# Scores of a graph-attention kernel: two pairs of groups by seven half-size products, one list of buffers, three paced queues

## The chip, the cores and the metric

One core of one Trainium2 chip. The metric is the device time of one execution in microseconds (us), given as the median of several runs. Where a ratio is given, it is the mean time of one kernel's fast runs over that of the other's fast runs of the same rounds, so it is not quite the ratio of the medians quoted beside it; the bracket behind it is a 95% interval.

## The reference, cut to what matters

```python
# layer 0: x = layernorm(x + relu(adj @ (max(sign(x), 0) @ sign(w0).T)))     x: 4096 x 512, adj: 4096 x 4096
node_att = softmax(x @ node_w, axis=0)
h = x @ edge_w
e = h @ h.T                                  # symmetric: block (A, B) is block (B, A) turned
e = where(adj > 0, e, NEG_BIG)
edge_att = softmax(e, axis=1)                # over rows: block (B, A) has its own minima and sums
output = adj * (node_att * edge_att) @ (x @ weight) + bias
# then layernorm(x + output)
```

The kernel cuts the 4096 rows into 8 groups of 512 (`NG = 8`, `W = 512`), each of four blocks of 128 rows (`BG = 4`). A pair (A, B) of groups is 512 x 512 scores. Only 28 pairs off the diagonal and 8 on it are multiplied; the mirror block is made by turning (transposing) on TensorE. This stage, the stage of the scores, is the one that is changed. It lasts a quarter of the run.

## The kernel before

The stage of the scores, with cuts marked. `later` is one queue of following work, of which four entries are emitted after each row.

```python
blk = ctx.enter_context(tc.tile_pool(name="blk", bufs=11))
adjp = ctx.enter_context(tc.tile_pool(name="adjp", bufs=2))
def some(n):
    for _ in range(min(n, len(later))):
        later.popleft()()
class Scores:
    # load(): two adjacency tiles of 128 x 2048, [...]
    def prepare(self):
        for a in self.a:
            nc.vector.tensor_scalar(a, a, 0.0, NEG_BIG, ALU.is_le, ALU.mult)      # L332
    def stats(self, a, i, r, c, s):                                             # one row block: mask, minimum, exp
        nc.vector.tensor_tensor_reduce(e, e, s, -1.0, HUGE, ALU.add, ALU.min, accum_out=nmax_c[...])
        later.append(lambda: nc.scalar.activation(e, e, AF.Exp, ...))
    def main(self):
        for i in range(BG):
            # four accumulating matmuls into pe (128 x 512 in PSUM)             # L356
            nc.scalar.copy(s[:, i, lo * P :], pe[:, lo * P :])                  # L363
            if not diag:
                self.stats(self.a[0], i, A, B, pe)
            some(4)
            later.appendleft(lambda i=i: self.turn(s, t, i))                    # turned one i later
```

The helper `seven` was there already (the stage of h and the aggregation use the same seven-product scheme):

```python
def m1(ps, q, c11, c12, c21, c22): nc.scalar.copy(c21, ps)
def u2(ps, q, c11, c12, c21, c22): nc.vector.tensor_add(c12, c21, ps)           # L104
def u3(ps, q, c11, c12, c21, c22):
    nc.vector.tensor_add(c22, c21, ps)                                          # L110
    nc.vector.tensor_add(c22, c22, banks[2][q])                                 # L111
    after(q, 3)
# m2: ScalarE copy; m4, m3: one VectorE addition each (L119, L123)
```

TensorE needs the PSUM bank that `u2` reads for a later product, and the turn of a row waits for `u3`'s result.

## Time and profile before

| | before |
|---|---|
| time, median of 4 runs | 2026.82 us (2026.47 to 2028.78) |
| stage of the scores (first score product to first aggregation product) | 514.2 us |
| instructions of that stage on TensorE x their rate | 507.5 us |
| TensorE idle in that stage | 4.5 us |
| from the first aggregation product to the end | 896.4 us |

The second part of the table is worked out from the trace: each TensorE instruction of the stage by its nominal spacing (0.43 us for one of 128 x 512, as eight take 3.44 us at full rate; for narrower ones the trace shows 0.32 us with 384 columns, 0.22 with 256 and 0.11 with 128), then the idle time that the trace gives, then a remainder (2.2 us), in which instructions ran below their rate.

### The profile page before, as it was taken

To read this page: it belongs to the slowest core of one execution; us is meant where nothing else is said; L and a number is where in the kernel's file an instruction comes from. 1 tells how busy PE (TensorE), PEld (TensorE's weight loads), DVE (VectorE), ACT (ScalarE), POOL (GpSimd) and SP (SyncE) were. 2 spreads that over 40 slices of the span, in tenths; PEclk is the share of its full clock that TensorE was granted. 3 is DMA by queue.
4 is the path that set the end of the run, shared out by engine and by line. 5 is a ranking of instruction groups with operands and counts; after the bars stand their busy time and mean duration, and the time that the engine had idled before them with its cause. 6 is when DMAs were issued, how large, how long until landed. Compare 5 with 4: busy or idle time off the path is not lost.

```text
span 2025.5 us, 17689 instructions
## 1 busy us (share of the span) xinstructions
PE 2004.4 (99%) x6268; PEld 1108.3 (55%) x6268; DVE 1243.5 (61%) x1759; ACT 691.5 (34%) x1195; POOL 401.5 (20%) x485
## 2 busy tenths in 40 slices
PE   9999999999999999999999999999999999999997
PEld 4888888888544454545555444444444444444443
DVE  3555555556534554445545897786759775977634
ACT  4333333333113666666666521131221220222100
POOL 0243333334300000000001111140124111321101
PEclk9999999999999999999999999999999999999999
DMA  9566566565009786867767887765666765685421
GB/s 328 186 220 203 196 216 210 201 209 173 29 0 351 260 302 229 308 231 272 280 257 265 330 329 258 250 248 198 249 237 251 260 246 201 227 283 201 172 70 62
DMA packets 118153, 455.73 MB, mean 225 GB/s; under 512 B 10288, under 2 KB 10288, under 8 KB 93488
## 3 DMA queue, kind: packets, MB, share of 16 engines
q0 software_dynamic: 48128, 241.20, 31.6%
q1 hardware_dynamic: 69360, 212.36, 31.6%
q8 instruction: 49, 0.80, 0.2%
q10 hardware_dynamic: 576, 1.05, 0.1%
q14 instruction: 40, 0.33, 0.0%
HBM read 355.99 MB, written 98.57 MB: 224 GB/s over the span
## 4 chain that ended last, share of the span: by engine, by line
PE 96%; DMA 3%; DVE 1%; ACT 0%; issue 0%; SPq 0%; ACTq 0%; POOLq 0%; POOL 0%; DVEq 0%
PE ps L479 38%; PE pe L356 21%; PE acc L209 11%; PE acc L208 11%; PE po L531 5%; PE seven L89 5%; PE pt L377 3%; DMA a<-in_adj_dram 2%; PE pw L181 1%; PE pt L238 1%; DMA xt<-in_x_t_dram 1%; DVE lo L205 0%; PE ptm L405 0%; DMA xb<-x_d 0%; ACT a L342 0%
## 5 line engine op out<-in xcount | busy, mean ns | idle before, releaser
L356 PE MATMUL pe<-hT 128*128 128x512 f32 (+3 forms) x1152 | 475.5, 557 | 0.0
L479 PE MATMUL ps<-q,lop 128*128 128x512 f32 x1024 | 446.9, 592 | 0.0
L208 PE MATMUL acc<-xw,hi 128*128 128x512 f32 x1024 | 401.6, 392 | 0.0
L209 PE MATMUL acc<-xw,lo 128*128 128x512 f32 x1024 | 399.4, 390 | 0.6 <-DVE lo L205 0.5
L479 PE MATMUL ps<-t,lop 128*128 128x512 f32 x768 | 332.9, 592 | 0.0
L479 PEld LDWEIGHTS ps<-q,lop 128*128 128x128 f32 x1024 | 193.9, 190 | 240.8 <-issue 237.0
L356 PEld LDWEIGHTS pe<-hT 128*128 128x128 f32 x1152 | 205.0, 191 | 184.0 <-issue 174.8
L434 ACT ACTIVATE q<-q 128x2048 f32<-128x2048 f32 x64 | 122.3, 1911 | 407.8 <-DVE q L431 394.2
L205 DVE TENSOR_TENSOR lo<-at,hi 128x1024 fp32r<-128x1024 f32 x128 | 168.7, 1318 | 147.1 <-ACT hi L203 147.1
L479 PEld LDWEIGHTS ps<-t,lop 128*128 128x128 f32 x768 | 145.9, 190 | 183.7 <-issue 180.3
L440 DVE SCALAR_TENSOR_TENSOR q<-ac,q 128x512 f32<-128x512 f32 x256 | 198.9, 830 | 53.6 <-ACT q L434 39.1
L203 ACT CAST hi<-at 128x1024 fp32r<-128x1024 f32 x128 | 134.6, 1052 | 272.6 <-PE acc L208 271.3
L209 PEld LDWEIGHTS acc<-xw,lo 128*128 128x128 f32 x1024 | 192.3, 188 | 41.0 <-DVE lo L205 1.7
L208 PEld LDWEIGHTS acc<-xw,hi 128*128 128x128 f32 x1024 | 192.3, 188 | 39.3
L338 DVE CUSTOM_DVE_ANT_0 a<-a,pe 128x512 f32<-128x512 f32 x112 | 76.7, 687 | 206.9 <-ACT s L363 206.9
L342 ACT ACTIVATE a<-a,nmax_c 128x512 f32<-128x512 f32 x256 | 183.5, 718 | 45.8 <-DVE nmax_c L338 45.5
L483 DVE TENSOR_TENSOR over<-over,ps 128x512 f32<-128x512 f32 x168 | 113.6, 681 | 107.8 <-PE ps L479 107.7
L431 DVE CUSTOM_DVE_ANT_1 q<-q,mrow 128x2048 f32<-128x2048 f32 x64 | 148.5, 2325 | 40.3 <-DMA q<-s_d 36.2
L363 ACT COPY s<-pe 128x512 f32<-128x512 f32 (+2 forms) x144 | 77.7, 543 | 138.4 <-PE pe L356 120.3
L531 PE MATMUL po<-over 128*128 128x512 f32 x256 | 115.9, 600 | 3.7 <-DVE xb L540 3.7
L425 POOL DMA_DIRECT2D ac<-in_adj_t_dram x64 | 48.8, 763 | 325.3 <-DVE q L440 253.4
L377 PEld LDWEIGHTS pt<-ident,s 128*128 128x128 f32 x496 | 62.1, 141 | 68.7 <-issue 57.7
(107 smaller groups left out, 1553.8 us busy)
## 6 DMA issues: line engine op xcount, KB each, us to landing
at<-in_adj_t_dram SPq DMA_DIRECT2D x64, 1024.0 KB, 5.1
ac<-in_adj_t_dram POOLq DMA_DIRECT2D x64, 1024.0 KB, 6.7
a<-in_adj_dram SPq DMA_DIRECT2D x64, 1024.0 KB, 7.5
q<-s_d POOLq DMA_DIRECT2D x64, 1024.0 KB, 7.8
lop<-lop_d SPq DMA_DIRECT2D x112, 512.0 KB, 4.1
s_d<-s POOLq DMA_DIRECT2D x36, 1024.0 KB, 4.8
s_d<-t POOLq DMA_DIRECT2D x28, 1024.0 KB, 6.2
xb<-in_x_dram SPq DMA_DIRECT2D x32, 256.0 KB, 3.1
```

What stands on the lines that cost most here:

```text
L203: nc.scalar.copy(hi, aq)
L205: nc.vector.tensor_sub(lo, aq, hi.bitcast(F32))
L208: nc.tensor.matmul(acc, hi[:, c, :], xw[:, kb, :], start=(kb == 0), stop=False)
L209: nc.tensor.matmul(acc, lo[:, c, :], xw[:, kb, :], start=False, stop=(kb == NB - 1))
L342: lambda: nc.scalar.activation(e, e, AF.Exp, bias=nmax_c[:, b, c : c + 1], scale=-1.0, accum_out=sum_c[:, b, c : c + 1])
L356: nc.tensor.matmul(pe[:, lo * P :], hT[:, k, ts(A * BG + i, P)], hT[:, k, (B * BG + lo) * P : (B + 1) * W], start=(k == 0), stop=(k == KD ...
L377: nc.tensor.transpose(pt[:, j, :], s[:, i, ts(j, P)], ident)
L431: nc.vector._custom_dve(TENSOR_ADD_SAT, out=q, in0=q, in1=mrow.unsqueeze(1).to_broadcast([P, BG, W]), s0=0.0, s1=-HUGE)
L434: nc.scalar.activation(q, q, AF.Exp)
L440: nc.vector.scalar_tensor_tensor(qc, a[:, :, c, :], 0.0, qc, ALU.max, ALU.mult)
L479: nc.tensor.matmul(ps, lop[:, c, ts(h, P)], rop[m][:, c, :], start=(c == 0), stop=(c == BG - 1))
L531: nc.tensor.matmul(po, (lower if k // 2 else upper)[:, k % 2, ts(i, P)], w1_s[:, k, :], start=(k == 0), stop=(k == KD - 1),)
```

## The change

Two pairs (A, B) and (A, B+1) are made together by seven products of half size with five additions out of PSUM per half, instead of eight products. That saves TensorE one instruction in eight. The sums of the left and right operands are made by GpSimd. Eleven plus two buffers become one list of 13 that are handed back by count; the one queue `later` becomes three (turns, rows, exps), from which `tick` emits a little after every half product. The preparation of a tile is no longer emitted one unit ahead but directly ahead of the tile's first row. The core of the diff:

```diff
-    blk = ctx.enter_context(tc.tile_pool(name="blk", bufs=11))
-    adjp = ctx.enter_context(tc.tile_pool(name="adjp", bufs=2))
+    free = deque(slots_p.tile([P, BG, W], F32, name=f"slot{n}") for n in range(13))
+    def tick():
+        now[0] += 1
+        if turns and turns[0][0] <= now[0]:
+            turns.popleft()[1]()
+        for _ in range(1 + (len(stats) > 6)):
+            if stats:
+                stats.popleft()()
+        for _ in range(1 + (len(exps) > 4)):
+            if exps and exps[0][0] <= now[0]:
+                exps.popleft()[1]()
[...]
+        def row(self, i, s):
+            if self.fresh:
                 nc.vector.tensor_scalar(a, a, 0.0, NEG_BIG, ALU.is_le, ALU.mult)
+                self.fresh = False
             nc.vector.tensor_tensor_reduce(e, e, s.buf[:, i, :], -1.0, HUGE, ALU.add, ALU.min, ...)
[...]
+        def written(self, i):
+            stats.append(lambda: self.here.row(i, self.s))
+            turns.append((now[0] + 2, lambda: self.turn(i)))
[...]
+    class Couple:
+        def operands(self):
+            if B not in Couple.right:            # once per column of couples, 128 x 1024 each
+                nc.gpsimd.tensor_sub(t1, r12, r11)
+                nc.gpsimd.tensor_sub(t2, r22, t1)
+                nc.gpsimd.tensor_sub(t3, r22, r12)
+                nc.gpsimd.tensor_sub(t4, r21, t2)
+            nc.gpsimd.tensor_add(s1, l21, l22)   # per couple, 128 x 512 each
+            nc.gpsimd.tensor_sub(s2, s1, l11)
+            nc.gpsimd.tensor_sub(s3, l11, l21)
+            nc.gpsimd.tensor_sub(s4, l12, s2)
+        def main(self, between):
+            seven(left, right, [...], follow)
[...]
+    for B in range(0, NG, 2):
+        units += [Couple(A, B) for A in range(B)]
+        units += [Single(B, B), Single(B, B + 1), Single(B + 1, B + 1)]
```

## The prediction

What it calls the lock is this, in the trace of the kernel before: four operations of VectorE that read two SBUF operands (L440) took 9.33 us beside three GpSimd operations of 6.94 us together, and 2.48 us without them. The name stands for these longer durations; what causes them, no trace shows.

> **What bounds the kernel now.** I read the page first (busy shares, slices, chain), then the stage of the scores by windows, then its timeline instruction by instruction, then the waits of the other engines.

> ```profile
> span 2025.5 us, 17689 instructions
> PE 2004.4 (99%) x6268; PEld 1108.3 (55%) x6268; DVE 1243.5 (61%) x1759; ACT 691.5 (34%) x1195; POOL 401.5 (20%) x485
> PEclk9999999999999999999999999999999999999999
> PE 96%; DMA 3%; DVE 1%; ACT 0%; issue 0%; SPq 0%; ACTq 0%; POOLq 0%; POOL 0%; DVEq 0%
> L356 PE MATMUL pe<-hT 128*128 128x512 f32 (+3 forms) x1152 | 475.5, 557 | 0.0
> 614.90:1129.20 514.30, 509.85 (x1652) 262.42 (x1651) 260.53 (x615) 329.16 (x783) 39.40 (x72) 1.00 0.76 278
> ```

> TensorE works without a break (99%, full clock) and the chain is TensorE for 96%. The last line is the window of the score stage: length, then busy PE, weight loads, DVE, ACT, POOL, clock, DMA share, GB/s. 509.85 of 514.30 us are TensorE; DVE is at 51%, ACT at 64%. A busy TensorE need not be at its rate, so the timeline decides:

> ```profile
> 800.84 3.60 PE L356 MATMUL pe<-hT 128*128 128x512 f32 x8
> 804.27 0.60 PE L377 MATMUL pt<-ident,s 128*128 128x128 f32 x4
> 804.71 3.60 PE L356 MATMUL pe<-hT 128*128 128x512 f32 x8
> ```

> One product of 128x512 is two instructions (1152 = 2 x 576 products). Eight of them start 3.43 us before the transposes that follow, and the windows 663 to 741 and 741 to 1104 are busy to the last hundredth (78.00 of 78.00, 363.00 of 363.00): 0.429 us per instruction is the rate, and the time goes down only with the number of instructions. The only idle of TensorE in the stage is at its start, 2.91 and 1.54 us (waits on ACT's copy, which stood behind DVE and the first adjacency loads):

> ```profile
> 639.33 1.14 PE L377 MATMUL pt<-ident,s 128*128 128x128 f32 x8 [2.91 <-ACT s L363]
> 659.22 0.66 PE L377 MATMUL pt<-ident,s 128*128 128x128 f32 x4 [1.54 <-ACT s L363]
> ```

> [...] in the aggregation stage:

> ```profile
> 1334.34 9.33 DVE L440 SCALAR_TENSOR_TENSOR q<-ac,q 128x512 f32<-128x512 f32 x4 [1.05 <-DMA ac<-in_adj_t_dram]
> 1334.36 6.94 POOL L504 TENSOR_TENSOR over<-over 128x1024 f32<-128x1024 f32 x3
> L213 DVE CUSTOM_DVE_ANT_0 scr<-xb,nw_b x32: 693/1246/1251, 56.3 to 522.6; 128x512 f32<-128x512 f32 x32
> ```

> Four operations that elsewhere take 2.48 us together took 9.33 us, longer by just about the 6.94 us of three POOL operations; DVE did not get in between them. L213 is the row operation of the score stage in form, and doubles (693 to 1246 ns) beside POOL. [...] Here a 128x512 subtraction took 1306 ns on POOL alone (L262) and 0.69 us on DVE: 1.9x. [...] a ready copy stood behind an exp that waited for DVE.

> **The change, part by part.** *Products.* There are 28 pairs off the diagonal and 8 on it. The new order makes 12 couples (2+4+6) out of 24 pairs; 4 pairs and the diagonal stay. Two pairs cost 2 x 16 = 32 products; seven products of half size are 7 x 2 x 2 = 28, at the same width of 512. Saved: 4 products, 8 instructions x 0.429 = 3.43 us per couple, x 12 = **41.2 us**, 96 instructions. All of it lies on the path. The transposes stay (496). A couple takes 56 x 0.429 = 24.0 us and eight groups of transposes at 0.44 us = 3.5 us: 27.5 us, where two pairs took 8 x 3.87 = 31.0 us. Floor: 2026.6 - 41.2 = 1985.4 us, a ratio of 0.980.

> *DVE.* Each couple adds ten additions out of PSUM (five per half). Such an addition is 0.69 us, 0.61 back to back by the same helper in the stage of h (L104 to L123 show 688, 687, 686, 687, 684 ns). Rows come every 0.615 us back to back (starts 798.00, 798.62, 799.23, 799.84), a tile's preparation is 1.22 us (L332). Per couple: 16 x 0.615 + 4 x 1.22 + 10 x 0.61 = 20.8 us of 27.5, 76%; two pairs had 14.7 of 31.0, 47%.

> *POOL.* Each couple needs four sums of 128x512, about 1.3 us each: 5.2 us. Each of three new columns (B = 2, 4, 6) needs four more of 128x1024, 2.34 us each (the fastest of L273): 9.4 us. None had to be made before. All 16 rows of a couple now read two SBUF operands (half read PSUM before)[...]: 20.8 + 5.2 = 26.0 us of 27.5, 95%.

> *ACT.* It loses four of eight copies per couple (-2.3 us): 16 exps at 0.705 (starts 798.84, 799.55, 800.25), 8 turn copies at 0.59, 4 copies at 0.58 make 18.3 us of 27.5, 67%. Not a bound.

> *Slack.* Before, a row was turned one i later, 3.4 us after its product ended, and only an ACT copy lay between. Now it is turned one half-product later, 1.72 us, and six of eight rows come through DVE. For the row of the fourth product two additions must fit: product's end + 0.2 us (in the stage of h the additions start at 539.61 and 543.05, their products end at 539.41 and 542.85) + 1.3 us = 1.5 us. With a free DVE it fits by some 0.2 us. With DVE behind it doesn't, and TensorE waits in order.

> *Buffers.* 11 + 2 buffers of 8 KB per partition become one list of 13; a couple holds about nine at once. In the aggregation this loads the masks two at a time as before, and TensorE had no idle there: I expect 0 there.

> **What is given back (estimates).** Placing the queues by hand: the stores of a pair come a few half-products before the sums in POOL's order, so the sums run roughly around half-products 4 to 8, when DVE has rows and preparations and then the two tight pairs of additions. Of 5.2 us of lock, DVE's idle takes most; I count 1 us of TensorE wait per couple: **+12 us**. At a new column POOL's chain to the second product's operands (four of 2.34, two of 1.3: 12 us) starts in the diagonal unit before it, some 9 us before TensorE needs it, and earlier as far as POOL runs ahead; DVE is held out meanwhile. 2 us each: **+6 us**. At the change of stage the first block's q load is issued one step before its shift; in-order DVE and ACT would stand behind a load (7.8 us median landing) that was issued 9 to 13 us ahead before (1095.44 and 1099.91 for a shift at 1108.86). The products' copies wait behind that: **+4 us**. The start has two loads before it instead of four, and the first unit waits for one tile: of the 4.45 us idle perhaps **-3 us** (some comes back). Sum: 1985.4 + 12 + 6 + 4 - 3 = 2004; I take **2003 us**, 1.2% less.

> **Rivals.** (A) *All of it arrives*: 1985 us, or 1983 with the better start. For it: every engine but TensorE stays under its capacity, the row queue is bounded and doubles its pace above six, and the 5.2 us of POOL may fall into DVE's idle; the same seven products ran in the stage of h at 0.429 us per instruction. Against it: there DVE had little else to do. (B) *DVE under the lock becomes the bound*: if sums block DVE right ahead of additions, each couple loses 2.5 us or more, 30 us, and the columns and the change of stage 15 to 20: 2020 to 2030 us, nothing gained. For it: 95% and 9.33 us for 2.48 us of work above. Against: a TensorE wait lets DVE catch up[...]. (C) *Buffers or transfers*: with 13 buffers taken, emission must drain queues early and loads wait for exps; the same bytes in 473 us make 302 GB/s where the stage had 278 and single slices 351. It would show as DVE waiting for in_adj; some us at most.

> **Range and chances.** A and B bracket the result; the paced queues speak for the better half, the lock for the worse. 1986 to 2020 us should hold it 8 times in 10. Faster by over 2% means under 1986.1 us, which needs the whole floor: 0.14. Slower by over 2% would need more than 80 us of new stalls: 0.03. Within 2%: 0.83.

> **What would show it.** Right: 1056 instructions in the two score lines together (672 more on the helper's L89 row), and the stage's window about 490 us; busy DVE there near 340 us plus time in which rows last over 1 us beside POOL; TensorE idle, ended by DVE additions, ahead of transposes in the couples. Step "lock" is wrong if rows stay at 687 ns or if no TensorE idle follows; "columns" is wrong if TensorE has no gap at the first couples of a column; "change of stage" is wrong if TensorE runs through from the last score into the first block. A time under 1988 us means that slack was enough; one above 2020 us that DVE paces the couples.

## More of the kernel before

The prediction shows the main lines. Two more are needed later. The list of waits has one for VectorE (the columns: waiting line, releaser, us in total, times, longest):

```profile
DVE a L332 <- DMA a<-in_adj_dram: 27.8, 17, 10.8
```

and the page's list of transfers gives what an adjacency tile takes from issue to landing (last number, us):

```profile
a<-in_adj_dram SPq DMA_DIRECT2D x64, 1024.0 KB, 7.5
```

So VectorE already stood 27.8 us, up to 10.8 us at a time, with a preparation at the head of its queue whose tile had not landed. It cost TensorE only the 4.5 us at the start of the stage; after that TensorE never came to wait for VectorE here.

## The result, and the profile after

The changed kernel takes **2097.92 us** (median of 4, 2096.48 to 2100.87) against 2026.82 us, ratio 1.0351 [1.0333, 1.0369]: 3.5% slower, outside the predicted range of 1986 to 2020 us. From the page of the changed kernel:

```profile
span 2099.1 us, 17645 instructions
...
PE 2003.9 (95%) x6170; PEld 1101.2 (52%) x6172; DVE 1340.2 (64%) x1879; ACT 663.1 (32%) x1147; POOL 507.4 (24%) x545
...
PEclk9999999999999998899998999999999999999999
...
PE 81%; DMA 11%; DVE 4%; ACT 3%; issue 1%; POOL 0%; POOLq 0%; DVEq 0%; SPq 0%
...
L359 DVE TENSOR_SCALAR slot<-slot 128x2048 f32<-128x2048 f32 x64 | 90.6, 1417 | 146.2 <-DMA slot<-in_adj_dram 146.0
...
slot<-in_adj_dram SPq DMA_DIRECT2D x64, 1024.0 KB, 12.1
```

Before, the chain that ended last was TensorE for 96% and the clock line (PEclk: the clock that TensorE was granted, in tenths of full speed) had only nines. Now the chain is TensorE for 81%, transfers for 11% and VectorE for 4%; TensorE is idle at times, and the clock line has eights where it had been full. L359 is the preparation of an adjacency tile: VectorE stands 146.0 us in front of it, waiting for the tile to land. The waits, by line:

```profile
DVE slot L359 <- DMA slot<-in_adj_dram: 146.0, 44, 8.6
...
PE seven L89 <- DVE slot L104: 47.1, 12, 7.7
...
PE pt L410 <- DVE slot L111: 17.5, 9, 3.0
...
PE pt L410 <- ACT slot L445: 12.4, 3, 4.6
```

TensorE waits 47.1 us for the additions of `u2`, 17.5 us for those of `u3`. The stage as a window (length, busy PE, PEld, DVE, ACT, POOL, then clock, DMA share and GB/s):

```profile
616.00:1203.50 587.50, 508.89 (x1561) 255.31 (x1560) 364.90 (x737) 302.99 (x739) 131.13 (x130) 0.93 0.65 242
```

| us | before | after | difference |
|---|---|---|---|
| stage of the scores | 514.2 | 587.5 | +73.3 |
| its TensorE instructions at their rate | 507.5 | 467.0 | -40.5 |
| TensorE idle in it | 4.5 | 78.6 | +74.1 |
| remainder: below the rate | 2.2 | 41.9 | +39.7 |
| from there to the end | 896.4 | 895.5 | -0.9 |

So the products were saved as predicted and the aggregation is as it was. (The table has 40.5 us for the predicted 41.2 because six transposes of the kernel before come after its first aggregation product, and so outside the stage; with them it is 41.2.) The loss is TensorE idle and, after it, slow TensorE. One couple shows how (columns: start, duration in us, engine, line, operation, count, and in brackets the idle time before and what ended it):

```profile
1050.01 1.23 DVE L359 TENSOR_SCALAR slot<-slot 128x2048 f32<-128x2048 f32 x1 [2.59 <-DMA slot<-in_adj_dram]
...
1053.60 0.68 DVE L104 TENSOR_TENSOR slot<-slot,seven 128x512 f32<-128x512 f32 x1
...
1057.66 2.50 DVE L359 TENSOR_SCALAR slot<-slot 128x2048 f32<-128x2048 f32 x1 [3.38 <-DMA slot<-in_adj_dram]
...
1060.08 0.67 DVE L104 TENSOR_TENSOR slot<-slot,seven 128x512 f32<-128x512 f32 x1
1060.68 1.21 DVE L359 TENSOR_SCALAR slot<-slot 128x2048 f32<-128x2048 f32 x1
...
1060.81 3.67 PE L89 MATMUL seven<-right,slot 128*128 128x512 f32 x4 [3.45 <-DVE slot L104]
...
1065.35 1.23 DVE L359 TENSOR_SCALAR slot<-slot 128x2048 f32<-128x2048 f32 x1 [3.46 <-DMA slot<-in_adj_dram]
...
1068.04 1.09 PE L410 MATMUL pt<-ident,slot 128*128 128x128 f32 x4 [2.69 <-DVE slot L111]
```

Read it from the middle. The second L104 addition stands behind a preparation. VectorE is idle for 3.38 us because the preparation's tile lands late; the preparation takes 2.50 us (beside a GpSimd sum, 1.22 otherwise); then comes the addition, and TensorE, idle for 3.45 us, goes on 0.7 us after the addition began. Its next four instructions then start 0.85 to 0.90 us apart, where 0.43 is the rate: they run at half rate. The same follows at 1065.35 for `u3`.

Nothing written says that this preparation comes before this addition. In the text of the program it stands directly ahead of its tile's first row. In the order in which the built program holds VectorE's instructions it does not (the number, line and operation of the couple shown above; rows shortened to `L362`, and what each preparation is for added behind it):

```
953 L359 preparation of slot10    its first row is number 1000: 16 rows and 10 additions later
954, 956, 958, 960  L362 rows of slot0
962 L104 addition (u2)
963 L359 preparation of slot11    first row 988: 7 rows and 8 additions later
964 L104 addition (u2)            <- TensorE waits for this one
965 L359 preparation of slot4     first row 1021: 18 rows and 14 additions later
966 L359 preparation of slot7     first row 1016: 16 rows and 13 additions later
967 L110 addition (u3)
968 L111 addition (u3)            <- and for this one
```

A preparation depends on nothing but its tile's load, and the build has put it far ahead. Over the 64 tiles it stands on average 13 rows and 8.3 additions ahead of its first row. In the kernel before it stood nearly 18 rows ahead, but with no addition between.

The loads themselves are not faster for it: they are issued when a buffer comes free, four loads and four stores close together. The window from 1028 to 1072 us in 40 slices, with the share of the DMA engines and their rate:

```profile
DMA  0000000000000899699999999999999991000000
GB/s 0 0 0 0 0 0 0 0 0 0 0 0 0 357 357 238 246 391 272 404 413 434 439 402 391 404 400 410 393 387 458 415 376 37 0 0 0 0 0 0
```

About 22 us at some 380 GB/s, then nothing: a tile lands 12.1 us after its issue (7.5 before), though the stage as a whole moves only 242 GB/s.

### The profile page after: what moved, and what is told of

Same layout as the page of the kernel before. It is cut to its first block, busy times and chain, and to the rows that moved or that the text cites. A ratio compares the mean times of both kernels' runs of the same rounds, so it can differ in the third digit from the quotient of the medians.

```text
span 2099.1 us, 17645 instructions
## 1 busy us (share of the span) xinstructions
PE 2003.9 (95%) x6170; PEld 1101.2 (52%) x6172; DVE 1340.2 (64%) x1879; ACT 663.1 (32%) x1147; POOL 507.4 (24%) x545
## 3 DMA queue, kind: packets, MB, share of 16 engines
q0 software_dynamic: 48128, 241.20, 30.4%
q10 hardware_dynamic: 576, 1.05, 0.1%
## 4 chain that ended last, share of the span: by engine, by line
PE 81%; DMA 11%; DVE 4%; ACT 3%; issue 1%; POOL 0%; POOLq 0%; DVEq 0%; SPq 0%
PE ps L604 37%; PE acc L209 11%; PE seven L89 11%; PE acc L208 11%; DMA slot<-in_adj_dram 10%; PE po L657 5%; PE pe L436 2%; ACT slot L368 2%; PE pt L410 2%; PE pw L181 1%; DVE slot L359 1%; DVE slot L362 1%; PE pt L238 1%; DMA s_d<-slot 1%; ACT slot L411 1%
## 5 line engine op out<-in xcount | busy, mean ns | idle before, releaser
L604 PE MATMUL ps<-slot,lop 128*128 128x512 f32 x1792 | 774.1, 592 | 0.0
L604 PEld LDWEIGHTS ps<-slot,lop 128*128 128x128 f32 x1792 | 339.9, 190 | 425.2 <-issue 414.2
L546 ACT ACTIVATE slot<-slot 128x2048 f32<-128x2048 f32 x64 | 122.0, 1911 | 394.1 <-DVE slot L543 394.1
L552 DVE SCALAR_TENSOR_TENSOR slot<-slot,slot 128x512 f32<-128x512 f32 x256 | 185.9, 779 | 51.2 <-DMA slot<-in_adj_t_dram 37.7
L368 ACT ACTIVATE slot<-slot,nmax_c 128x512 f32<-128x512 f32 x256 | 183.6, 720 | 108.2 <-DVE nmax_c L362 108.1
L362 DVE CUSTOM_DVE_ANT_0 slot<-slot,slot 128x512 f32<-128x512 f32 x256 | 181.3, 740 | 46.1 <-ACT slot L115 28.5
L543 DVE CUSTOM_DVE_ANT_1 slot<-slot,mrow 128x2048 f32<-128x2048 f32 x64 | 158.0, 2473 | 68.0 <-DMA slot<-s_d 66.8
L89 PE MATMUL seven<-right,slot 128*128 128x512 f32 x288 | 143.9, 652 | 47.1 <-DVE slot L104 47.1
L359 DVE TENSOR_SCALAR slot<-slot 128x2048 f32<-128x2048 f32 x64 | 90.6, 1417 | 146.2 <-DMA slot<-in_adj_dram 146.0
L436 PE MATMUL pe<-hT 128*128 128x512 f32 (+3 forms) x384 | 135.0, 500 | 0.0
L89 PEld LDWEIGHTS seven<-right,slot 128*128 128x128 f32 x288 | 57.1, 204 | 122.8 <-issue 65.2
L411 ACT COPY slot<-pt 128x512 f32<-128x512 f32 (+3 forms) x136 | 73.9, 546 | 131.4 <-PE pt L410 110.9
## 6 DMA issues: line engine op xcount, KB each, us to landing
slot<-in_adj_dram SPq DMA_DIRECT2D x64, 1024.0 KB, 12.1
```

The costliest lines, as they stand in the source:

```text
L89: nc.tensor.matmul(banks[bank][q], lop(m, q)[k], rop(m)[k], start=(first and k == 0), stop=(k == K - 1), skip_group_check=not first,)
L362: nc.vector.tensor_tensor_reduce(e, e, s.buf[:, i, :], -1.0, HUGE, ALU.add, ALU.min, accum_out=nmax_c[:, b, c : c + 1])
L368: nc.scalar.activation(e, e, AF.Exp, bias=nmax_c[:, b, c : c + 1], scale=-1.0, accum_out=sum_c[:, b, c : c + 1])
L436: nc.tensor.matmul(pe[:, lo * P :], hT[:, k, ts(p.A * BG + i, P)], hT[:, k, (p.B * BG + lo) * P : (p.B + 1) * W], start=(k == 0), stop=(k ...
L543: nc.vector._custom_dve(TENSOR_ADD_SAT, out=q, in0=q, in1=mrow.unsqueeze(1).to_broadcast([P, BG, W]), s0=0.0, s1=-HUGE)
L552: nc.vector.scalar_tensor_tensor(qc, a[:, :, c, :], 0.0, qc, ALU.max, ALU.mult)
```

## The experiments

Three explanations were open after this reading. **Order**: the preparations stand ahead of TensorE's additions in VectorE's queue, and wait there for their tiles (3.38 us in the couple above, with TensorE idle for 3.45). **Lock**: VectorE's operations last longer beside GpSimd's sums, as the preparation of 2.50 us above (the prediction's main loss). **Supply**: 13 buffers or the transfers are too few. All medians are in us; "before" ran in the same rounds (2026.6 to 2028.2 us). The experiments were made in four sets of rounds on four chips (e1 to e4, e5 to e8, e9 to e11, e12 and e13), so a difference between runs of different sets is uncertain by some 1.5 us.

| run | edit | median | ratio to before | idle + remainder of the stage |
|---|---|---|---|---|
| after | | 2097.92 | 1.0351 [1.0333, 1.0369] | 78.6 + 41.9 |
| e1_pin_prep | preparation kept in written order | 2033.81 | 1.0034 [1.0019, 1.0049] | 37.6 + 17.1 |
| e2_thin_sums | short GpSimd sums | 2100.66 | 1.0357 [1.0340, 1.0374] | 79.1 + 41.6 |
| e3_singles | no couples | 2039.24 | 1.0063 [1.0048, 1.0078] | 7.8 + 7.7 |
| e4_slots14 | a 14th buffer | 2089.74 | 1.0307 [1.0292, 1.0322] | 80.2 + 27.2 |
| e5_pin_turn3 | e1 and a later turn | 2015.27 | 0.9934 [0.9919, 0.9948] | 23.0 + 11.5 |
| e6_pin_thin_sums | e1 and e2 | 2009.00 | 0.9904 [0.9887, 0.9920] | 20.4 + 10.2 |
| e7_turn3 | later turn alone | 2111.18 | 1.0408 [1.0392, 1.0423] | 90.2 + 42.6 |
| e8_pin_singles | e1 and e3 | 2022.67 | 0.9971 [0.9956, 0.9986] | 0.6 + 1.0 |
| e9_pin_turn3_pool | e5, GpSimd in written order | 2034.57 | 1.0037 [1.0023, 1.0052] | 38.4 + 17.6 |
| e10_turn4_pool_first | e9, turn later still, next stage's loads earlier | 2017.14 | 0.9950 [0.9934, 0.9967] | 30.0 + 9.8 |
| e11_turn3_pool_rows_first | e9, rows in written order, loads earlier | 2031.55 | 1.0026 [1.0009, 1.0042] | 36.9 + 12.3 |
| e12_dve_sums | e5, all sums on VectorE | 1988.23 | 0.9802 [0.9789, 0.9816] | 7.3 + 5.9 |
| e13_dve_sums_turn2 | e1, all sums on VectorE | 1989.08 | 0.9803 [0.9791, 0.9815] | 5.0 + 4.8 |

### e1_pin_prep: the preparation alone in its written place

```diff
-                nc.vector.tensor_scalar(a, a, 0.0, NEG_BIG, ALU.is_le, ALU.mult)
+                tc.keep_in_program_order(nc.vector.tensor_scalar(a, a, 0.0, NEG_BIG, ALU.is_le, ALU.mult))
```

> One edit: each preparation of an adjacency tile (one DVE operation on 128x2048) is pinned behind what was written before it on DVE, so that it stands right ahead of its own first row (0.2 rows and 0.5 additions between, mean of 64) and not 13.1 rows and 8.3 additions ahead of it, where the compiler's scheduler put it. Theory ORDER (DVE waits in order at a hoisted preparation for a tile that has not landed, and the additions behind it hold TensorE): 1985 to 2005 us, DVE's wait for in_adj in the score stage from 146 us to under 30, additions no longer end TensorE's idle. Rival LOCK (the POOL sums shut DVE out): over 2070 us. Rival BUFFERS (13 buffers too few, tiles simply come too late): over 2060 us, the wait for in_adj stays over 80 us and only stands ahead of other rows.

Measured: 2033.81 us, 64.1 us less than the changed kernel, by this one line, though not the 1985 to 2005 us that I expected: additions still end TensorE's idle time, those of `u3`. In its built order a preparation is 0.2 rows ahead of its first row on average. Its waits:

```profile
PE pt L410 <- DVE slot L111: 31.0, 9, 5.4
DVE slot L359 <- DMA slot<-in_adj_dram: 5.1, 1, 5.1
```

The 146.0 us of VectorE's waits for tiles are 5.1, with the same buffers and nearly the same landing time (11.9 us), and TensorE no longer waits for L104 at all. So the tiles were not late for their rows, only for the places at which the build had put their preparation. What remains, 31.0 us for L111, is another thing. The same place of a couple in this run:

```profile
1009.17 1.26 POOL L473 TENSOR_TENSOR slot<-hT 128x512 f32<-128x512 f32 x1 [5.55 <-PE seven L89]
...
1009.35 1.62 DVE L362 CUSTOM_DVE_ANT_0 slot<-slot,slot 128x512 f32<-128x512 f32 x1
...
1012.08 1.72 POOL L474 TENSOR_TENSOR slot<-slot,hT 128x512 f32<-128x512 f32 x1
...
1012.59 1.75 DVE L362 CUSTOM_DVE_ANT_0 slot<-slot,slot 128x512 f32<-128x512 f32 x1
...
1014.27 1.90 DVE L362 CUSTOM_DVE_ANT_0 slot<-slot,slot 128x512 f32<-128x512 f32 x1
...
1016.10 1.22 DVE L359 TENSOR_SCALAR slot<-slot 128x2048 f32<-128x2048 f32 x1
...
1017.24 0.68 DVE L110 TENSOR_TENSOR slot<-slot,seven 128x512 f32<-128x512 f32 x1
1017.95 0.69 DVE L111 TENSOR_TENSOR slot<-slot,seven 128x512 f32<-128x512 f32 x1
...
1018.78 1.09 PE L410 MATMUL pt<-ident,slot 128*128 128x128 f32 x4 [2.81 <-DVE slot L111]
```

Rows of 0.69 us take 1.15 to 1.90 us beside GpSimd's sums (1.62, 1.15, 1.75 and 1.90 for the four) and push the two tight additions back; TensorE waits 2.81 us. This is the mechanism of the prediction's rival B, and the time is near the 2020 to 2030 us that it gave.

### e2_thin_sums and e6_pin_thin_sums: the lock, with and without the pin

```diff
+            w = 8 if A else P
-            nc.gpsimd.tensor_add(s1, l21, l22)
+            nc.gpsimd.tensor_add(s1[..., :w], l21[..., :w], l22[..., :w])
             # the other three sums of a couple likewise
```

This makes wrong operands in the couples with A above 0 (the comparison let the result pass, so it can't be used to check such a kernel). The four sums of a couple stay in GpSimd's queue with their waits, but last a fraction.

> The order of DVE is as in the changed kernel, but the four POOL sums of a couple are made on 8 of 128 columns (not for the three first couples); results are wrong on purpose. The POOL time of a couple falls from 5.3 us to about 1. ORDER: 2075 to 2100 us. LOCK: under 2050 us. BUFFERS: 2085 to 2100 us.

Measured: 2100.66 us, no gain at all, with 79.1 us idle as in the changed kernel. As long as the preparations set VectorE's pace, the lock is not what ends last. Together with the pin of e1:

> Preparations pinned as in e1, and the POOL sums on 8 of 128 columns as in e2 (wrong operands on purpose). SLACK-AND-LOCK: without the lock the rows ahead of the first pair of additions take 0.69 us again, DVE is 3 us or more earlier there, the pauses go: 1988 to 2004 us, where the same edit gained nothing (2100.7) with hoisted preparations. Rival (throughput of DVE or the preparation alone): over 2020 us.

Measured: 2009.00 us, 24.8 us below e1, but above the 1988 to 2004 us that I expected. The same edit is worth nothing in one order and 25 us in the other. The trace says where the rest is: of e1's eight pauses of over 2 us for L111, the six of 2.6 to 4.8 us are gone or under 0.8 us, and the two of 5.4 us stand as they were, 5.45 and 5.44 us, beside the sums of 128 x 1024 for the next column, which this edit left at full size.

### e3_singles and e8_pin_singles: the rest of the change without couples

```diff
-        units += [Couple(A, B) for A in range(B)]
+        units += [Single(A, C) for A in range(B) for C in (B, B + 1)]
```

> The new queues, list of 13 and order of units, but every pair by itself with full products (no couples, no sums, no additions out of PSUM). Preparations are hoisted as far as in the changed kernel (16.3 rows). ORDER: nothing that TensorE needs stands behind them except ACT's exps, so 2020 to 2040 us, near the kernel before. LOCK: the same, 2020 to 2030. BUFFERS: the list and the queues cost by themselves, over 2050 us.

Measured: 2039.24 us. Every pair is multiplied in the old way here, with the new queues and the list of 13.

> Every pair by itself as in e3_singles (2039.2 us, 12 above the kernel before), preparations pinned. If those 12 us come from exps and copies on ACT that stand behind rows behind hoisted preparations: 2024 to 2031 us. If the one list of 13 or the pace of the queues costs them: 2036 to 2042 us.

Measured: 2022.67 us. The moved preparations cost even this order 16.6 us; with the pin, queues and buffers by themselves are 0.3% better than the kernel before, with only 0.6 us of TensorE idle in the stage. The buffers and queues by themselves are thus not the fault.

### e4_slots14: one buffer more

```diff
-    free = deque(slots_p.tile([P, BG, W], F32, name=f"slot{n}") for n in range(13))
+    free = deque(slots_p.tile([P, BG, W], F32, name=f"slot{n}") for n in range(14))
-        mrow = pan.tile([P, W], F32, name="mrow")
+        mrow = pan.tile([P, W], F32, name="mrow", bufs=2)
```

> A 14th buffer in the list (room from two of four mrow buffers), nothing else. BUFFERS: under 2065 us, as each tile can be asked for earlier. ORDER: hoisting stays (13.8 rows); loads come a little earlier, 2070 to 2098 us. LOCK: 2090 to 2100 us.

Measured: 2089.74 us, 8.2 us less. VectorE still waits 119.5 us for tiles. Supply is a small part. (The room came from two buffers of the aggregation, which took 898.0 us here against 895.5. Twelve buffers can't be tried: the program's list then never has one free where it needs it, and the build doesn't end.)

### e5_pin_turn3 and e7_turn3: more slack for the turn

```diff
-            turns.append((now[0] + 2, lambda: self.turn(i)))
+            turns.append((now[0] + 3, lambda: self.turn(i)))
```

The turn of a row comes three half products after it, not two. With the pin:

> Preparations pinned as in e1_pin_prep, and each row turned one half-product later (now + 3 for now + 2). In e1 TensorE still stood 31.4 us in 12 pauses of about 2.6 us, one per couple, at the transposes of the first row with two additions; DVE was late there by four rows of 1.15 to 1.90 us beside the four POOL sums and by one preparation. Theory SLACK-AND-LOCK: 2.15 us more slack leaves about 0.5 us of each pause and ends most of the half-clock time after it: 1988 to 2004 us, idle in the score stage under 15 us. Rival: the pauses come from DVE's throughput (additions, rows and preparations over a whole couple), then they only move: over 2020 us.

Measured: 2015.27 us, 18.5 us below e1 and better than both kernels, but above what I expected, with 23.0 us idle. (Nor was it one pause per couple in e1: its trace has eight for L111 of over 2 us, of 2.6 to 5.4, in the 12 couples.) Without the pin:

> The later turn alone, preparations hoisted as in the changed kernel (12.9 rows, 7.7 additions ahead). ORDER: the pauses of 4 to 8 us at additions that stand behind a late tile stay, 2070 to 2098 us. If slack alone were the cause: under 2050 us.

Measured: 2111.18 us, outside what I expected, and 13 us worse than the changed kernel. The additions still stand behind preparations whose tiles have not landed; TensorE waited 60.7 us for L111 here (17.5 before the edit). Why it got worse rather than stayed equal I did not follow further.

### e9, e10, e11: trying to keep GpSimd's sums where they were written

The largest pauses left in e5 were two of 4.9 us, at the last couple of a column, where rows ran beside GpSimd's sums for the next column's right operands. I took their place to be the trouble, and pinned all GpSimd sums to their written order:

```diff
-                nc.gpsimd.tensor_sub(t1, r12, r11)
+                tc.keep_in_program_order(nc.gpsimd.tensor_sub(t1, r12, r11))
                 # and so for all eight GpSimd sums                           (e9, e10, e11)
-            turns.append((now[0] + 3, lambda: self.turn(i)))
+            turns.append((now[0] + 4, lambda: self.turn(i)))               # e10
-            nc.vector.tensor_tensor_reduce(
+            tc.keep_in_program_order(nc.vector.tensor_tensor_reduce(       # e11
```

e10 and e11 also emit the first loads of the next stage ahead of its two panels.

> As e5_pin_turn3 (2015.3 us), and the POOL operations that make a column's and a couple's operands are pinned behind what was written before them on POOL, so that the four of 128x1024 of the next column leave the last couple of the column before, where each held a row for 2.7 us. If the two pauses of 4.9 us (at 696 and 852 us in e5) are theirs: both gone, 2003 to 2010 us, the seven small pauses of 1.3 us stay. If not theirs: 2013 to 2017 us.

> Preparations and POOL operands pinned, rows turned two half-products later than in the changed kernel (now + 4), and the first block's loads asked for ahead of the two panels. The pauses of 1.3 us per couple fall to 0, and the pause of 3.4 us where ACT stands behind the first block's shift, which waits for its load, falls by the two steps (3.5 us): score stage within 8 us of its 467 us of instructions, 1988 to 1998 us. If later turns bring waits of their own (buffers held longer): over 2003 us.

> As e10 with now + 3, and the row operations pinned too, so that no row stands between the two additions of a pair. If the 1.3 us pauses come from that row (0.6 us) and the preparation ahead (1.2 us) together with the lock: the pauses shrink to about 0.7 us, 1992 to 2003 us; if pinning rows makes DVE wait for something later: over 2010 us.

Measured: 2034.57, 2017.14 and 2031.55 us. None beats e5, against what I expected. In e9 the two pauses of 4.9 us are gone, and two of 7.4 us stand in the single pairs after them, waiting for ScalarE's copies (L411); the small ones grew from 1.35 to 2.25 us. In e10 a pause of 9.8 us appeared at the change of stage. Moving the sums about only moved the collision.

### e12_dve_sums and e13_dve_sums_turn2: no GpSimd arithmetic in the stage

```diff
-            nc.gpsimd.tensor_add(s1, l21, l22)
+            tc.keep_in_program_order(nc.vector.tensor_add(s1, l21, l22))
             # and so for all eight sums; the four left sums come three half products later than before,
             # into a buffer that is taken where it was
```

> The pinned preparation with the later turn (2015 us) once more, but with the four sums of a couple that GpSimd makes, two left sums and two right operands, made by VectorE instead, kept in their written places; GpSimd then does no arithmetic in the score stage. They cost VectorE about 2.8 us per couple beside its 20.8, so 23.6 of 27.5 us. Theory A: what is left of TensorE's pauses (1.35 us per couple and 4.9 us at the last two couples of a column) comes from the shared lock, VectorE's rows and additions lasting up to 2.8 and 1.9 us beside the GpSimd sums. Then those rows go back to 0.8 to 1.1 us and the time falls to 1995 to 2008 us, near what I predicted blind. Theory B: the pauses come from the order of VectorE's queue, whatever stands ahead of the additions; then the sums, four more things in that queue, lengthen them, and the time is 2015 us or over.

Two things in this expectation are not as the runs have them. All eight sums were moved, four left ones per couple and four right ones per column, as the edit says. And VectorE's additions out of PSUM lasted 0.69 us at most in e5; the long ones were rows (up to 2.84 us) and preparations (up to 3.06).

Measured: **1988.23 us** (1987.16 to 1992.20), 27.0 us below e5, below even the 1995 to 2008 us that the theory of the lock gave, though VectorE has more to do. What was still open was how far the later turn had a part in it:

> The version of 1988 us with only the turn put back to two half products after its row (in the version just run it was three). Theory L: the 26 us that were left after the pin (2034 against 1988 and the nominal 1985) are the shared lock nearly alone; without GpSimd sums two additions fit into 1.72 us with 0.2 us to spare as predicted, and this runs in 1988 to 1995 us. Theory S: the slack was the other half of it; with two half products any row, preparation or sum of up to 1.2 us that VectorE has just begun makes TensorE wait, some 0.5 to 1.2 us in each of the 12 couples with its slow instructions after it, and this runs in 1997 to 2012 us. The pinned kernel gained 18.5 us from the later turn while GpSimd still made the sums.

Measured: **1989.08 us** (1986.40 to 1991.26), which is e12 within the spread of both, and what theory L expected. So the pin and the absence of GpSimd sums are the whole matter, and the slack of two half products, the prediction's 0.2 us, was enough once nothing stretched VectorE's operations. The row operation L362 and the preparation L359, as groups with shortest, median and longest duration in ns, in e1:

```profile
L362 DVE CUSTOM_DVE_ANT_0 slot<-slot,slot x256: 662/687/2828, 627.8 to 1157.1; 128x512 f32<-128x512 f32 x128
...
L359 DVE TENSOR_SCALAR slot<-slot x64: 1215/1222/3358, 620.5 to 1149.6; 128x2048 f32<-128x2048 f32 x64
...
L111 DVE TENSOR_TENSOR slot<-slot,seven x24: 677/686/689, 662.0 to 1082.3; 128x512 f32<-128x512 f32 x24
```

and in e13:

```profile
L362 DVE CUSTOM_DVE_ANT_0 slot<-slot,slot x256: 665/685/697, 629.4 to 1112.7; 128x512 f32<-128x512 f32 x128
...
L359 DVE TENSOR_SCALAR slot<-slot x64: 1216/1221/1333, 621.9 to 1105.3; 128x2048 f32<-128x2048 f32 x64
...
L111 DVE TENSOR_TENSOR slot<-slot,seven x24: 679/686/687, 663.5 to 1038.3; 128x512 f32<-128x512 f32 x24
```

The medians are equal; what goes is the tail, 2828 to 697 ns and 3358 to 1333 ns. The additions out of PSUM (L111) have no tail in either (689 and 687 ns at most): what lasts longer in e1 are the rows, which read two SBUF operands, and the preparation, which reads one (2048 elements per partition in 1.22 us without the tail, against 512 in 0.61 for rows back to back). The waits of e13, and the window of the stage in e1 and then in e13:

```profile
PE pt L410 <- ACT slot L448: 3.9, 1, 3.9
...
PE pt L410 <- DVE slot L111: 1.0, 2, 0.6
```

```profile
614.60:1135.90 521.30, 483.72 (x1558) 248.32 (x1557) 374.94 (x725) 300.06 (x730) 141.11 (x130) 0.97 0.72 272
...
616.10:1092.60 476.50, 471.51 (x1559) 244.50 (x1558) 370.29 (x787) 300.30 (x730) 43.34 (x71) 0.99 0.79 298
```

In e13 TensorE is 471.51 of 476.50 us busy, GpSimd has only its transfers left (43.34 us, 141.11 in e1), and the same 13 buffers move 298 GB/s. A couple lasts 27.7 us on average to the start of the next (e5: 29.1, e1: 32.2, the changed kernel: 38.5; from the starts of their products, without the first and the last couple of each column; the first takes 27.3 to 27.8 us in all four kernels, but for one of 30.4). Two limits of this reading: moving the sums empties GpSimd's queue of them as well as ending the lock, so the stores behind them also go earlier; that the lock is the part that counts is shown by the durations above and by e6, which leaves queue and waits as they are, shortens only the sums of the couples, and loses the pauses beside these but not those beside the sums of the columns. In no trace did a product on TensorE wait for a GpSimd sum in this stage. And the gain of 2.0% lies on the line of 2%: the interval of e13 is 0.9791 to 0.9815.

## Why the prediction was wrong, by its own steps

*What bounds, and "Products".* Right. TensorE at its rate was the bound, and 96 instructions went, 41.2 us of nominal time.

*"Aggregation: I expect 0 there".* Right: 895.5 against 896.4 us.

*"Placing the queues by hand".* This step failed. I laid VectorE's queue out in the order in which the program writes it, each preparation directly ahead of its first row. The built program has it 13.1 rows and 8.3 additions earlier, and VectorE stood at preparations of tiles not yet landed, 146.0 us in all, with those additions behind them. That cost 64.1 us (e1), which no term of the sum held. The prediction even named a ready copy behind an exp that waited (TensorE idle for 2.91 and 1.54 us); it didn't ask whose order the queue has. Its sign for a time above 2020 us, "DVE paces the couples", would have misled: VectorE was busy for 364.9 of the stage's 587.5 us; it stood waiting in the wrong place.

*Rival (C), buffers or transfers.* It named the right sign, VectorE waiting for adjacency tiles, and the wrong size ("some us at most"; 146.0 us) as well as the wrong cause. 13 buffers and 298 GB/s do (e13; I had worked out 302), and a 14th buffer gives 8.2 us.

*"Lock", 12 + 6 us.* Right that it comes (rows of 0.69 us took up to 2.83 in e1), too small. From e1 to e13, which differ by the GpSimd sums alone (their engine, their being kept in written order, and the place of the left ones), it is 44.7 us. Per couple I counted 1 us of waiting; e1 shows six pauses of 2.6 to 4.8 us and two of 5.4 at the last couples of columns. I let the sums fall into VectorE's idle time; they fell onto rows, and each row then held the next back (1.62, 1.15, 1.75, 1.90 us in a run of four). Nor did I count what a pause does to TensorE afterwards: 17.1 us of the loss in e1, 41.9 in the changed kernel, are instructions below their rate.

The 95% counted too much under the lock: VectorE's ten additions of a couple, 6.1 of its 20.8 us, lasted 690 ns at most in e1, with GpSimd's sums still there. And rival (B), which came true once the order was mended, was summed up wrongly: 1985.4 + 30 + 15 to 20 makes 2030 to 2035 us and not 2020 to 2030; e1 took 2033.8.

*"Columns".* 2 us each predicted. The pauses were 5.45 and 5.44 us in e1, and in the couple before a new column rather than in the first of it, since these sums too were built earlier than written.

*"Slack", 0.2 us to spare.* Right: with two half products and no lock TensorE waits 1.0 us for L111 in the whole stage (e13).

*"Change of stage", 4 us.* Right: 3.7 us in e1, 3.9 in e13, and by the mechanism named, a copy of ScalarE (L445, L448) behind a shift that waited for its load.

*"Start", -3 us.* Near: the 4.5 us that the kernel before idled at its start are gone; the changed kernel's first pause of over 1 us comes at 689 us.

*The chances.* "Slower by over 2% would need more than 80 us of new stalls: 0.03". There were 74.1 us more idle and 39.7 us more below the rate. The 0.03 rested on the written order like everything else.

Put together: 2026.8 - 41.2 = 1985.6; e13 stands 2.2 us above its own such floor (1989.1 against 2028.1 - 41.2); the lock adds 44.7 and the order 64.1: 2096.6 us against 2097.9. The last two terms are differences of neighbouring runs, so the sum is a way to keep the books and no further proof. And the lock's share is that in the mended order; in the changed kernel itself it lay hidden behind the other (e2 gained nothing).

## What to carry to other kernels

Before placing queues by hand, look at the order in which the built program holds each engine's instructions: an operation that depends only on a load may have been moved far ahead, as the preparations here (13 rows and 8.3 additions), and VectorE then stood at it, its tile not landed, ahead of additions that TensorE waited for (3.45 us in the couple shown, 64.1 us of the kernel's time). A wait that costs next to nothing in the profile before (27.8 us here) becomes the first suspect when a change puts that engine on the critical path. And when two causes lie over one another, undoing the smaller alone shows nothing; undo the larger first, then try the smaller again, and where one engine's operations last longer beside another's (rows of 0.69 us up to 2.83 here), try the slower-looking choice of doing all the work on one (44.7 us from e1 to e13).
